# Biases as a feature of layer norm 2, and 64x64 quarters in the slice attention of a fused graph attention and slice attention kernel

## The chip, the cores and the metric

The kernel runs on one core of a Trainium2 chip. A core has four engines that compute, each with its own queue of instructions: TensorE (PE in the profile, with its weight loads as PEld), VectorE (DVE), ScalarE (ACT) and GpSimd (POOL). SyncE (SP) issues DMA transfers. Matmuls write to PSUM, the other tiles lie in SBUF. The metric is the device time of one execution in microseconds, and the median of several executions is given.

## The reference

The input `x` has 32 items of 512 nodes with 256 features, all float32. One layer is two blocks with a residual each. The first is a graph attention network on a layer norm of `x`. The second, which the change touches, is slice attention on a second layer norm:

```python
x = x + gnn(layernorm(x), adj, ...)        # MLP, attention without mask, MLP, attention with mask
x = x + ffn(layernorm(x), ...)

def layernorm(x):                          # over the 256 features
    return (x - mean(x)) / sqrt(var(x) + 1e-5)

def ffn(x, ...):                           # H = 8 heads, D = 64, G = 64 slices
    fx_mid = (x @ W_fx + b_fx)             # per head: [N, 64]
    x_mid  = (x @ W_x + b_x)
    slice_weights = softmax((x_mid @ W_slice + b_slice) / clip(temperature, 0.1, 5.0))
    slice_norm  = slice_weights.sum(over nodes)
    slice_token = einsum('bhnc,bhng->bhgc', fx_mid, slice_weights) / (slice_norm + 1e-5)
    q, k, v = slice_token @ W_q, slice_token @ W_k, slice_token @ W_v
    attn = softmax(q @ k.T / 8)
    out_x = einsum('bhgc,bhng->bhnc', attn @ v, slice_weights)
    return out_x @ W_out + b_out
```

A layer-normed row sums to zero. So its last feature is minus the sum of the 255 others, and a product with a weight matrix can do without it if the matrix's last row is subtracted from all rows.

## The kernel before

Every operation is recorded under a step name (`norm2`, `w`, `sums`, `tokens`, `att`, `vo`, `gg`, `out` for the second block), and a list scheduler in the kernel then orders the operations of all 32 items on each engine. `TURNS`, `PERIOD`, `HEAD` and `TAIL` are the numbers that rank the steps: the higher the turn, the later. Items overlap, so that one item's small steps stand between large matmuls of the others. `HEAD` and `TAIL` shift the first and the last three items. All operations come from one helper, so one source line stands for them all in the profile, and groups are told apart by their tiles.

W_slice and the temperature are folded into W_x (`weff`, with the bias `beff`), W_q and W_k into `wqk`, W_v and W_out into `wvo`. Heads are handled in pairs: 8 heads make 4 pairs of 2 x 64.

```python
# norm2
xn = new("xn2", [P, NT, D + 1])
nc.gpsimd.memset(xn[:, :, D : D + 1], 1.0)        # a column of ones behind the features
layernorm(x1, xn, "ln2")
# ... transposed to xnT ...

# w: for each of four tiles of 128 nodes
nc.tensor.matmul(pm, xnT[:, k, ts(t)], weff[:, k, :], ...)          # k = 0, 1
nc.vector.tensor_tensor(wt, pm, beff, op=OP.add)
nc.vector.tensor_reduce(mx, w3, axis=AX.X, op=OP.max)
nc.vector.tensor_tensor(w3, w3, mx[...].to_broadcast(...), op=OP.subtract)
nc.scalar.activation(wt, wt, AF.Exp)
# ... sum, reciprocal, product ...

# sums: for each pair of heads
nc.tensor.matmul(pm, w[:, t, ts(p)], xn[:, t, :], ...)              # 257 columns, t = 0..3
nc.vector.tensor_scalar(rn, pm[:, D : D + 1], 1e-5, None, op0=OP.add)
# ... s1 = pm / rn; then
pn = sm_tile([NP, P])
nc.tensor.transpose(pn, s1[:, :, D], ident)
for s in range(2):
    nc.vector.tensor_tensor(nrow[:NP, s], ident[...], pn[...], op=OP.mult)

# tokens: wfx times s1T, 16 matmuls of 128 rows x 64 columns; then b_fx
for a in range(2):
    for s in range(2):
        nc.tensor.matmul(pm[ts(s, C), a::2], bfx[:, ts(a, C)], nrow[:, s, a], ...)

def halves(dst, blocks, src):
    for p in range(NP):
        for s in range(2):
            nc.tensor.matmul(dst[ts(s, G), p, :], blocks[:, p, ts(s, G)], src[:, p, :], ...)

def diagonal(dst, src):
    nc.vector.tensor_copy(dst(0), src(0))
    nc.scalar.copy(dst(1), src(1))

nc.tensor.matmul(pq, wqk, tok, start=True, stop=True)
diagonal(... qbd ..., ... pq ...)
halves(psc, qbd, tok)
# att: softmax over psc into sc;  vo: tok and sc transposed
diagonal(... tokbd ..., ... pt ...)
halves(pa, tokbd, attT)
diagonal(... meanbd ..., ... pa ...)
# gg
for p2 in range(NP // 2):
    pg = mm_tile([P, 2, D])
    for s in range(2):
        p = 2 * p2 + s
        nc.tensor.matmul(pg[:, s, :], meanbd[:, p, :], wvo[:, p, :], start=True, stop=True)
    # ... gg = pg + bout
```

`qbd`, `tokbd` and `meanbd` are block-diagonal: zeroed once at the start, and in each item only the two 64x64 blocks of each pair are written. The matmuls contract over all 128 rows, half of which are zero.

Of the kernel before, what the change touches and what calls it, by code (L numbers as in the profile page):

```python
# [10 lines left out]
OP = mybir.AluOpType  # L11
# [5 lines left out]
    "load": -122.2, "norm1": 78.3, "mlp1": 267.5, "h": 296.1, "factors": 313.0, "p": 323.7,  # L17
    "pv": 324.8, "o1": 324.8, "mlp2": 340.5, "h2": 360.8, "e": 385.5, "p2": 385.7,
    "pv2": 430.7, "norm2": 437.4, "w": 494.8, "sums": 496.8, "s1T": 507.4, "tokens": 549.1,
    "att": 558.0, "vo": 558.2, "gg": 560.3, "out": 593.0,  # L20
}
PERIOD, SPARE = 91.1, 0.01

HEAD = (
    (6, -4, -3, 60, -53, 4, -23, -45, -472, 2, -221, -20, 5, -305, -38, -19, -41, -1, 1, -8, -195,
     -10),
    (30, 8, 50, 2, 2, -82, 15, -145, -199, -303, -27, 8, -12, -2, -60, -10, 0, 0, 67, 37, -53,
     -43),
    (0, 0, 24, -14, -200, -9, -14, 38, -69, -68, -93, -18, 33, 0, -64, 3, -16, -34, -14, 0, -61,
     0),  # L30
)
TAIL = (
    (-3, 1, 8, 12, -103, 59, 0, -11, -97, 0, 0, 24, -57, 61, 1, -29, -30, 0, 24, -32, -1, 2),
    (8, -26, 13, 11, -14, 15, 0, 7, -21, -8, -28, 44, -103, 6, -322, 16, 99, 21, 47, 130, 189,
     192),
    (3, 35, 0, 3, 5, 53, -42, 26, -5, 1, 12, -62, 128, 43, 54, -6, -1, -52, -9, -21, -32, -10),
# [7 lines left out]
P = 128  # L44
# [4 lines left out]
class Recorder:  # L49
# [39 lines left out]
    def take(self, engine, method, args, kwargs):  # L89
# [6 lines left out]
        op.half = engine == "tensor" and outs[0].ap[0][1] == P // 2  # L96
# [26 lines left out]
    def _cost(self, op, out, ins):  # L123
# [10 lines left out]
        if op.engine == "tensor":  # L134
            one = max(n / 1200 + 0.002, 0.109)
            if op.half:
                one = max(n / 2400, 0.038)
            return (one if op.method == "transpose" else 2 * one), self.DRAIN
# [13 lines left out]
    def _schedule(self, ops, key, spare):  # L152
# [34 lines left out]
        done, moved, half = [], 0.0, False  # L187
        while len(done) < len(ops):
# [21 lines left out]
            if op.engine == "tensor" and op.half != half:  # L210
                t, half = t + self.SWITCH, op.half
# [102 lines left out]
def adj_ffn_kernel(  # L314
# [61 lines left out]
    Q = 32  # L376
# [106 lines left out]
    bfx = new("bfx", [P, P])  # L483
    nc.gpsimd.memset(bfx, 0.0)
    nc.sync.dma_start(bfx[:NP], b_fx.rearrange("(p f) -> p f", p=NP))
    nrow = new("nrow", [P, 2, 2, NP // 2, G])
    nc.gpsimd.memset(nrow, 0.0)
# [10 lines left out]
    tokbd = new("tokbd", [P, NP, P])  # L498
    nc.gpsimd.memset(tokbd, 0.0)
    qbd = new("qbd", [P, NP, P])  # L500
    nc.gpsimd.memset(qbd, 0.0)
    meanbd = new("meanbd", [P, NP, P])
    nc.gpsimd.memset(meanbd, 0.0)

# [3 lines left out]
    beff = new("beff", [P, INNER])  # L508
# [47 lines left out]
    bxc = new("bxc", [P, NP])  # L556
    nc.sync.dma_start(bxc, b_x.rearrange("(m p) -> p m", p=P))
    bsl = new("bsl", [P, G])
    nc.sync.dma_start(bsl, bcast_dram(b_slice, G))
    for k in range(KD):  # L560
        pt = tr_tile([P, INNER])
        for p in range(NP):
            nc.tensor.transpose(pt[:, ts(p)], wx[:, k, ts(p)], ident)
        wxT = row("u")
        nc.scalar.copy(wxT, pt)
        pw = mm_tile([P, INNER])
        for p in range(NP):
            nc.tensor.matmul(pw[:, ts(p)], wxT[:, ts(p)], ws2, start=True, stop=True)
        nc.vector.tensor_tensor(
            weff[:, k, :].rearrange("p (h g) -> p h g", g=G),  # L570
            pw.rearrange("p (h g) -> p h g", g=G), rtemp_b, op=OP.mult,
        )
    pb = mm_tile([P, INNER])
    for p in range(NP):
        bxb = row("m", (P, P))
        nc.vector.tensor_copy(bxb, bxc[:, p : p + 1].to_broadcast([P, P]))
        nc.tensor.matmul(pb[:, ts(p)], bxb, ws2, start=True, stop=True)
    beff3 = beff.rearrange("p (h g) -> p h g", g=G)
    nc.vector.tensor_tensor(
        beff3, pb.rearrange("p (h g) -> p h g", g=G),  # L580
        bsl[:, None, :].to_broadcast([P, HEADS, G]), op=OP.add,
    )
    nc.vector.tensor_tensor(beff3, beff3, rtemp_b, op=OP.mult)
# [10 lines left out]
    nc.sync.dma_start(wo, W_out.rearrange("(k p) f -> p k f", p=P))  # L594
# [7 lines left out]
    def layernorm(src, dst, name):  # L602
# [9 lines left out]
        for t in range(NT):  # L612
            nc.vector.tensor_scalar(
                dst[:, t, :D], src[:, t, :], mv[:, t, 0:1], rstd[:, t : t + 1],
                op0=OP.subtract, op1=OP.mult,
            )
# [230 lines left out]
    def back(b, x1):  # L847

        nc.step = "norm2"
        xn = new("xn2", [P, NT, D + 1])  # L850
        nc.gpsimd.memset(xn[:, :, D : D + 1], 1.0)
        layernorm(x1, xn, "ln2")
# [16 lines left out]
        for t in range(NT):  # L869
            pm = mm_tile([P, INNER])  # L870
            for k in range(KD):
# [5 lines left out]
            nc.vector.tensor_tensor(wt, pm, beff, op=OP.add)  # L877
            mx = small("mx", [P, HEADS])
            nc.vector.tensor_reduce(mx, w3, axis=AX.X, op=OP.max)
            nc.vector.tensor_tensor(  # L880
                w3, w3, mx[:, :, None].to_broadcast([P, HEADS, G]), op=OP.subtract
# [18 lines left out]
        s1 = new("s1", [P, NP, D + 1])  # L900
        if by_dma("s1", b):
            stage = new("s1_stage", [P, D // Q, P], tag="stage4")
        for p in range(NP):
            pm = mm_tile([P, D + 1])
# [5 lines left out]
            nc.vector.tensor_scalar(rn, pm[:, D : D + 1], 1e-5, None, op0=OP.add)  # L910
            nc.vector.reciprocal(rn, rn)
            nc.vector.tensor_scalar(s1[:, p, :], pm, rn, None, op0=OP.mult)
            if by_dma("s1", b):
                flip(s1[:, p, :D], stage[:, :, ts(p, Q)])

        pn = sm_tile([NP, P])
        nc.tensor.transpose(pn, s1[:, :, D], ident)
        for s in range(2):
            nc.vector.tensor_tensor(
                nrow[:NP, s], ident[:NP, None, s:NP:2, None].to_broadcast([NP, 2, 2, G]),  # L920
                pn.rearrange("j (a o g) -> j a o g", a=2, o=1).to_broadcast([NP, 2, 2, G]), op=OP.mult,
            )
# [22 lines left out]
        pm = mm_tile([P, NP, G])  # L945
        for p in range(NP):
            for k in range(KD):
                for s in range(2):
                    pair, a = p // 2 * 2 + s, p % 2
                    nc.tensor.matmul(  # L950
                        pm[ts(s, C), p, :].rearrange("c (a i) -> c a i", i=Q),
                        wfx[:, k, ts(2 * pair + a, C)],
                        s1T[:, k, :].rearrange("p (a n i) -> p n a i", n=NP, i=Q)[:, pair, ts(a, 2)],
                        start=(p == 0 and k == 0), stop=False,
                    )
        for a in range(2):
            for s in range(2):
                nc.tensor.matmul(
                    pm[ts(s, C), a::2], bfx[:, ts(a, C)], nrow[:, s, a], start=False, stop=(a == 1)
                )  # L960
        nc.joint = False

        def halves(dst, blocks, src):

            nc.joint = True
            for p in range(NP):
                for s in range(2):
                    nc.tensor.matmul(
                        dst[ts(s, G), p, :], blocks[:, p, ts(s, G)], src[:, p, :],
                        start=True, stop=True,  # L970
                    )
            nc.joint = False

        def diagonal(dst, src):
            nc.vector.tensor_copy(dst(0), src(0))
            nc.scalar.copy(dst(1), src(1))

        tok = new("tok", [P, NP, G])
        nc.vector.tensor_copy(tok, pm)
        pq = mm_tile([P, NP, G])  # L980
        nc.tensor.matmul(pq, wqk, tok, start=True, stop=True)
        diagonal(lambda s: qbd[ts(s, C), :, ts(s, G)], lambda s: pq[ts(s, C), :, :])
        psc = sm_tile([P, NP, G])
        halves(psc, qbd, tok)
        nc.step = "att"
        amax = small("amax", [P, NP])
        nc.vector.tensor_reduce(amax, psc, axis=AX.X, op=OP.max)
        sc = new("sc2", [P, NP, G])
        nc.vector.tensor_tensor(
            sc, psc, amax[:, :, None].to_broadcast([P, NP, G]), op=OP.subtract  # L990
        )
        nc.scalar.activation(sc, sc, AF.Exp, scale=C ** -0.5)
        ra = small("ra", [P, NP])
# [3 lines left out]
            sc, sc, ra[:, :, None].to_broadcast([P, NP, G]), op=OP.mult  # L997
# [3 lines left out]

        pt = tr_tile([P, NP, C])
        for q in range(NP // 2):
            nc.tensor.transpose(pt[:, ts(q, 2), :], tok[:, ts(q, 2), :], ident)
        diagonal(lambda a: tokbd[ts(a, G), :, ts(a, C)], lambda a: pt[ts(a, G), :, :])
        pt = tr_tile([P, NP, G])
        for q in range(NP // 2):
            nc.tensor.transpose(pt[:, ts(q, 2), :], sc[:, ts(q, 2), :], ident)
        attT = new("attT", [P, NP, G], tag="sc2")
        nc.scalar.copy(attT, pt)  # L1010
        pa = mm_tile([P, NP, G])
        halves(pa, tokbd, attT)
        diagonal(lambda s: meanbd[ts(s, C), :, ts(s, G)], lambda s: pa[ts(s, C), :, :])
        nc.step = "gg"
        gg = med("gg")
        for p2 in range(NP // 2):
            pg = mm_tile([P, 2, D])
            for s in range(2):
                p = 2 * p2 + s
                nc.tensor.matmul(pg[:, s, :], meanbd[:, p, :], wvo[:, p, :], start=True, stop=True)  # L1020
# [86 lines left out]
```

## Time and profile before

| | |
|---|---|
| median of 3 executions | 2642.68 us (2642.13 to 2643.70) |
| granted TensorE clock, mean | 0.996 |
| TensorE idle before its first matmul | 8.65 us |
| DMA, mean rate | 142 GB/s |

In a line of a group stand: source line, engine, operation, tiles (written, then read), shape, count, then the time in which at least one of them ran, the mean duration of one, and the engine's idle time just before them with what ended it. A line of the timeline has the start, the time to the last end, the engine, the operation and its count. The recorded duration of a matmul contains its way through the pipeline, so that successive matmuls overlap.

### The profile page before, as it was taken

How to read it: one execution, taken by the hardware profiler on the slowest of the kernel's cores; microseconds unless marked ns; L12 is line 12 of the kernel's file. 1: busy time of each engine (PE TensorE's matmuls, PEld its weight loads, DVE VectorE, ACT ScalarE, POOL GpSimd, SP SyncE). 2: the span in 40 equal slices, each digit the busy share in tenths (PEclk: the TensorE clock that was granted, in tenths of full speed). 3: DMA queues.
4: the chain of work that ended last, by engine and by line, in shares of the span. 5: the costliest groups of instructions: out<-in, count | busy, mean ns of one | idle time of the engine just before them, and what ended most of it. 6: DMA issues, size and time to landing. Idle time of an engine off the chain costs nothing.

```text
span 2642.6 us, 35411 instructions
## 1 busy us (share of the span) xinstructions
PE 2601.8 (98%) x12477; PEld 1927.5 (73%) x12477; DVE 2093.8 (79%) x5161; ACT 1082.1 (41%) x2009; POOL 91.2 (3%) x171
## 2 busy tenths in 40 slices
PE   7999999999999999999999999999999999999998
PEld 5777777776777777777777777777777777777775
DVE  6578777987778877779877788877798777898785
ACT  3443444433444434444434444344444334443342
POOL 1000000000000000000000000000000000000000
PEclk9999999999999999999999999999999999999998
DMA  5135455544455554555545555545554545654441
GB/s 164 45 89 154 111 161 169 167 145 133 131 166 168 147 153 126 147 170 167 144 140 139 152 168 152 158 127 143 170 161 143 149 130 152 173 155 143 117 118 37
DMA packets 465658, 375.42 MB, mean 142 GB/s; under 512 B 86596, under 2 KB 382664, under 8 KB 465480
## 3 DMA queue, kind: packets, MB, share of 16 engines
q1 hardware_dynamic: 463896, 372.10, 49.4%
q8 instruction: 99, 1.62, 0.2%
q10 hardware_dynamic: 1584, 1.05, 0.1%
q14 instruction: 79, 0.65, 0.1%
HBM read 197.96 MB, written 175.11 MB: 141 GB/s over the span
## 4 chain that ended last, share of the span: by engine, by line
PE 75%; DVE 12%; DMA 8%; ACT 3%; issue 1%; SPq 1%; DVEq 0%; ACTq 0%
PE mm L277 72%; PE tr L277 3%; DMA w_raw<-scr 3%; DVE pT L277 2%; DMA o1T<-scr 2%; DMA scr<-u_stage 2%; ACT m L277 1%; DVE s L277 1%; DVE s_stage L277 1%; DVE w L277 1%; ACT acb L277 1%; SPq L277 1%; DVE u L277 1%; DVE w_stage L277 1%; DVE acb L277 1%
## 5 line engine op out<-in xcount | busy, mean ns | idle before, releaser
L277 PE MATMUL mm<-wfc,o0T 128*128 128x257 f32 x2048 | 495.6, 381 | 0.0
L277 PE MATMUL mm<-h,pT 128*128 128x256 f32 (+1 forms) x2048 | 466.8, 382 | 8.5 <-DVE pT L277 8.4
L277 PEld LDWEIGHTS mm<-h,pT 128*128 128x128 f32 x2048 | 381.5, 190 | 81.0 <-DVE pT L277 20.4
L277 PEld LDWEIGHTS mm<-wfc,o0T 128*128 128x128 f32 x2048 | 377.9, 189 | 83.7 <-issue 36.1
L277 PE MATMUL mm<-xn,w 128*128 128x257 f32 x1024 | 250.2, 380 | 1.5 <-DVE w L277 1.5
L277 ACT COPY h<-mm 128x257 f32<-128x257 f32 (+1 forms) x384 | 143.1, 373 | 257.8 <-PE mm L277 254.5
L277 PE MATMUL mm<-gg,wT 128*128 128x256 f32 x1024 | 248.5, 379 | 0.0
L277 PE MATMUL mm<-h,p2T 128*128 128x257 f32 x1024 | 241.8, 380 | 0.0
L277 PE MATMUL mm<-xnT,w 128*128 128x512 f32 x512 | 240.1, 602 | 1.0 <-ACT xnT L277 1.0
L277 PE MATMUL mm<-weff,xn2T 128*128 128x512 f32 x512 | 232.7, 596 | 0.0
L277 PE MATMUL mm<-o1T,w 128*128 128x512 f32 x512 | 226.8, 595 | 4.8 <-DVE o1T L277 4.6
L277 PEld LDWEIGHTS mm<-gg,wT 128*128 128x128 f32 x1024 | 191.7, 190 | 36.7 <-issue 12.4
L277 PEld LDWEIGHTS mm<-h,p2T 128*128 128x128 f32 x1024 | 193.3, 189 | 29.1 <-issue 0.6
L277 PEld LDWEIGHTS mm<-xn,w 128*128 128x128 f32 x1024 | 189.3, 190 | 30.9 <-ACT wT L277 1.3
L277 ACT ACTIVATE w<-w 128x512 f32<-128x512 f32 x128 | 80.6, 630 | 307.3 <-DVE w L277 307.1
L277 ACT ACTIVATE u<-mm,rd 128x256 f32<-128x256 f32 x192 | 89.6, 467 | 269.5 <-PE mm L277 149.0
L277 PEld LDWEIGHTS mm<-o1T,w 128*128 128x128 f32 x512 | 95.9, 190 | 116.6 <-issue 87.7
L277 DVE STREAM_TRANSPOSE o_stage<-o2T 128x512 f32<-128x512 f32 x64 | 45.2, 709 | 166.8 <-ACT o2T L277 166.8
L277 PEld LDWEIGHTS mm<-weff,xn2T 128*128 128x128 f32 x512 | 95.6, 191 | 98.0 <-issue 87.6
L277 DVE SCALAR_TENSOR_TENSOR e<-tr,h,mbias 128x512 f32<-128x512 f32 x120 | 86.4, 740 | 98.6 <-PE tr L277 98.6
L277 DVE SCALAR_TENSOR_TENSOR u<-m,u 128x512 f32<-128x512 f32 x192 | 129.7, 686 | 35.0 <-ACT m L277 33.5
L277 PEld LDWEIGHTS mm<-xnT,w 128*128 128x128 f32 x512 | 92.7, 191 | 86.5 <-issue 71.1
(151 smaller groups left out, 3769.8 us busy)
## 6 DMA issues: line engine op xcount, KB each, us to landing
scr<-xn_stage SPq DMA_DIRECT2D x240, 128.0 KB, 2.8
scr<-u_stage SPq DMA_DIRECT2D x120, 256.0 KB, 4.1
o1T<-scr SPq DMA_DIRECT2D x30, 1024.0 KB, 5.7
scr<-e_stage SPq DMA_DIRECT2D x120, 256.0 KB, 3.8
p2T<-scr SPq DMA_DIRECT2D x30, 1024.0 KB, 5.7
scr<-w_stage SPq DMA_DIRECT2D x120, 256.0 KB, 4.5
w_raw<-scr SPq DMA_DIRECT2D x30, 1024.0 KB, 6.3
x<-in_x_dram SPq DMA_DIRECT2D x32, 512.0 KB, 5.4
```

Source lines behind the costliest of these rows:

```text
L277: getattr(getattr(self.nc, op.engine), op.method)(*op.args, **op.kwargs)
```

## The change

Three things are done together. First, the normalised rows keep 255 features, and the last of the 256 becomes a one. `W_fx` and `W_x` have their last row subtracted from all rows in the setup, and their last row is then replaced by the bias. So the biases come with the product: `beff`, `bfx`, `nrow`, the transpose of the norms and the 257th column go. Second, the attention among slices and the product with W_v W_out work on 64x64 quarters of TensorE's array, without the block-diagonal tiles and their zeros. Third, the scheduler's numbers are new, and it knows the quarters as a mode of their own.

```diff
 TURNS = {
-    "load": -122.2, "norm1": 78.3, "mlp1": 267.5, "h": 296.1, ...
+    "load": -742.6, "norm1": -217.3, "mlp1": 743.3, "h": 847.3, ...
 }
-PERIOD, SPARE = 91.1, 0.01
+PERIOD, SPARE = 91.72, 0.01
 # ... HEAD and TAIL: all new
+    def less_last(w, source, bias):
+        last = row("m")
+        nc.sync.dma_start(last, bcast_dram(source[D - 1], INNER))
+        for k in range(KD):
+            nc.vector.tensor_tensor(w[:, k, :], w[:, k, :], last, op=OP.subtract)
+        nc.sync.dma_start(w[P - 1 : P, KD - 1, :], bias.rearrange("(p f) -> p f", p=1))
+    less_last(wfx, W_fx, b_fx)
 # ... and less_last(wx, W_x, b_x); setup of bfx, nrow, beff, bxc, the block-diagonal tiles: gone
-        xn = new("xn2", [P, NT, D + 1])
-        nc.gpsimd.memset(xn[:, :, D : D + 1], 1.0)
-        layernorm(x1, xn, "ln2")
+        xn = new("xn2", [P, NT, D])
+        nc.gpsimd.memset(xn[:, :, D - 1 : D], 1.0)
+        layernorm(x1, xn, "ln2", D - 1)
-            nc.vector.tensor_tensor(wt, pm, beff, op=OP.add)
-            nc.vector.tensor_reduce(mx, w3, axis=AX.X, op=OP.max)
+            nc.vector.tensor_reduce(mx, pm3, axis=AX.X, op=OP.max)
             nc.vector.tensor_tensor(
-                w3, w3, mx[:, :, None].to_broadcast([P, HEADS, G]), op=OP.subtract
+                w3, pm3, mx[:, :, None].to_broadcast([P, HEADS, G]), op=OP.subtract
             )
-            pm = mm_tile([P, D + 1])
+            pm = mm_tile([P, D])
-        pn = sm_tile([NP, P])
-        nc.tensor.transpose(pn, s1[:, :, D], ident)
-        for s in range(2):
-            nc.vector.tensor_tensor(nrow[:NP, s], ...)
-        for a in range(2):
-            for s in range(2):
-                nc.tensor.matmul(
-                    pm[ts(s, C), a::2], bfx[:, ts(a, C)], nrow[:, s, a], start=False, stop=(a == 1)
-                )
-        def halves(dst, blocks, src):
-        ...
-        def diagonal(dst, src):
-        ...
+        q = new("q", [P, 2, 2, G])
+        nc.scalar.copy(q, pq)
+        def quarters(dst, left, right):
+            nc.joint = True
+            for j in range(2):
+                for r in range(2):
+                    for c in range(2):
+                        nc.tensor.matmul(
+                            dst(r, c, j), left(r, c, j), right(r, c, j), start=True, stop=True
+                        )
+            nc.joint = False
+        psc = [sm_tile([P, 2, G]) for s in range(2)]
+        quarters(
+            lambda s, a, d: psc[s][ts(a, G), d, :],
+            lambda s, a, d: q[ts(s, C), a, d, :],
+            lambda s, a, d: tok[ts(s, C), a, d, :],
+        )
 # ... the softmax in two halves up to its exponential; tokT and attT transposed whole
+        pa = [mm_tile([P, 2, G]) for d in range(2)]
+        quarters(
+            lambda d, a, s: pa[d][ts(a, C), s, :],
+            lambda d, a, s: tokT[ts(d, G), a, ts(s, C)],
+            lambda d, a, s: attT[ts(d, G), s, ts(a, G)],
+        )
+        mean = new("mean", [P, 2, 2, G])
+        nc.vector.tensor_copy(mean[:, 0], pa[0])
+        nc.scalar.copy(mean[:, 1], pa[1])
-        for p2 in range(NP // 2):
-            pg = mm_tile([P, 2, D])
-            for s in range(2):
-                p = 2 * p2 + s
-                nc.tensor.matmul(pg[:, s, :], meanbd[:, p, :], wvo[:, p, :], start=True, stop=True)
+        pg = [mm_tile([P, 2, D]) for a in range(2)]
+        quarters(
+            lambda a, s, d: pg[a][ts(s, G), d, :],
+            lambda a, s, d: mean[ts(a, C), d, s, :],
+            lambda a, s, d: wvo[ts(a, C), 2 * d + s, :],
+        )
```

In `quarters`, `r` is the half of the array's rows and `c` the half of its columns. Each row half writes a PSUM tile of its own.

## The prediction

> **What bounds the kernel now.** I read the page's busy shares first, then the chain that ended last.
>
> ```profile
> PE 2601.8 (98%) x12477; PEld 1927.5 (73%) x12477; DVE 2093.8 (79%) x5161; ACT 1082.1 (41%) x2009; POOL 91.2 (3%) x171
> ...
> PE 75%; DVE 12%; DMA 8%; ACT 3%; issue 1%; SPq 1%; DVEq 0%; ACTq 0%
> ```
>
> TensorE (PE) is busy 98% of the span and makes up 75% of the chain. A busy PE could still be a slow one, so I looked at when its instructions start. Each fp32 matmul stands in the trace as two passes. Inside a run of equal passes the median distance of two starts is 216 ns at 257 columns, 429 ns at 512 and 109 ns for a 128-column transpose: all are columns / 1.2 GHz plus about 2 ns. In a steady item PE does nothing but stream, and what the change is worth is the PE time it takes out. VectorE (79%) and ScalarE (41%) have room. The same transpose of two successive items starts at 1303.91 and 1384.48 us: 80.6 us an item, 32 items 2578 us, the rest being head and tail.
>
> Next the groups by shape that the change touches (count, then busy us, mean ns):
>
> ```profile
> L277 PE MATMUL mm<-wvo,meanbd 128*128 128x256 f32 x256 | 72.7, 390 | 0.3 <-ACT meanbd L277 0.3
> L277 PE MATMUL mm<-s1T,wfx 128*64 128x64 f32 x1024 | 37.4, 226 | 3.7 <-DMA s1T<-scr 3.7
> L277 PE MATMUL tr<-tok,qbd 128*64 128x64 f32 x512 | 23.3, 231 | 1.6 <-DVE qbd L277 1.4
> L277 PE MATMUL mm<-attT,tokbd 128*64 128x64 f32 x512 | 21.9, 228 | 0.5 <-ACT attT L277 0.5
> L277 PE MATMUL mm<-nrow,bfx 128*64 128x128 f32 x256 | 20.3, 278 | 0.1
> ...
> L277 PE MATMUL tr<-ident,s 128*4 128x128 f32 x32 | 8.7, 271 | 0.0
> ```
>
> The mean of one (222 to 390 ns) contains the pipeline's latency, so the cost is not count times mean. It is the distance from one start to the next, which the timeline of one steady item gives (start us, then us from the first start to the last end):
>
> ```profile
> 1319.28 1.15 PE L277 MATMUL mm<-s1T,wfx 128*64 128x64 f32 x32
> 1320.26 0.61 PE L277 MATMUL mm<-nrow,bfx 128*64 128x128 f32 x8
> 1320.80 2.84 PE L277 MATMUL mm<-xnT,w 128*128 128x512 f32 x6
> ...
> 1325.72 0.69 PE L277 MATMUL tr<-tok,qbd 128*64 128x64 f32 x16
> 1326.33 0.44 PE L277 MATMUL tr<-ident,tok 128*128 128x128 f32 x2
> ...
> 1332.53 0.69 PE L277 MATMUL mm<-attT,tokbd 128*64 128x64 f32 x16
> 1333.15 1.13 PE L277 MATMUL mm<-wfc,o0T 128*128 128x257 f32 x4
> ```
>
> The 16 passes on qbd hold PE from 1325.72 to 1326.33, 0.61 us. Their single starts alternate 7 and 52 ns apart: the left and the right half of the array start 7 ns apart, and the next pair follows when the first has streamed its 64 columns. So 15 distances take 0.46 us, and the last one, on leaving for a 128x128 pass, 0.15. Entering a half-array group costs the pass before it a median 96 ns more than its columns, leaving one 99 ns more: about 0.195 us a visit, 99 visits in the run.
>
> **What the Trainium skill says.** "TensorEngine Tiling (Array Packing)", Key Properties: 64x64 gives four tiles that load weights and multiply independently, and a change of tiling mode drains TensorE. The trace agrees for two tiles (7 ns between the halves' starts) and puts the drain at 0.195 us a visit; no run here shows four tiles yet. "TensorE: Matmul & The Clock Gate", Part 3, has a pack span of one matmul plus about 4 ns per further tile; here it is 7 per tile. "TensorEngine Tiling (Array Packing)", Gotcha 1, says that different row tiles must not access one PSUM bank at the same time. The changed code gives each row half its own PSUM tile (`psc[s]`, `pa[d]`, `pg[a]`), so the four can overlap; before shows no row tiles. "TensorE: Matmul & The Clock Gate", Part 1, says that an idle PE falls to a lower clock; the tail of before shows it (0.72, below).
>
> **The change part by part, per item.**
> 1. Bias matmuls `nrow x bfx`: 8 passes go. Their pairs start 105 ns apart, 4 x 105 = 0.42, and with the step into them 0.44 us. The leaving switch now follows the tokens, so it is not saved.
> 2. The transpose of the norms (`s`, 4 columns of weights): 109 ns, 0.11 us.
> 3. `qbd` halves become `q` quarters: 16 passes remain, but four tiles run. Rounds of four: 4 x 52 ns, plus 3 x 7 ns within the last round, is 0.18 to the last start, plus 0.15 to leave: 0.35 instead of 0.61. Saved 0.26.
> 4. `tokbd` halves become `tokT` quarters: the same, 0.26.
> 5. Gates `meanbd x wvo`: 8 passes on the full array over block-diagonal weights of which half is zero. They start a mean 233 ns apart (216, and 320 where the weights were waited for): 1.87. After: 16 quarter passes of 256 columns in four rounds of 213 ns, 0.85, plus 0.02 of stagger, plus a new visit, 0.195: 1.07. Saved 0.80. This is the largest term and the least tested one.
> 6. Sums with 256 instead of 257 columns: 32 passes x 0.8 ns, 0.03.
>
> Sum 1.90 us an item, 61 us for 32 items. All of it lies on PE, which has no slack, so all of it should count.
>
> Off the path: VectorE loses the 128 additions of `beff` (84.8 us), 64 `nrow` products (24.3), and `qbd` and `tokbd` copies (13.2 + 13.0) in the whole run, while the subtraction and the maximum now read PSUM. In the profile reductions and additions of the same 512 columns take 663 to 683 ns whether from PSUM or SBUF, so this is free. VectorE comes to about 1970 us, even further from being the bound; the 0.33 us for pT that 25 items wait for it may shrink.
>
> **The new turns.** The order of instructions in the changed program shows the steady item much as before, with tighter fits behind the small groups: one 512-column matmul (0.86 us) between the q product and the quarters that need it (0.43 us for the product's own two passes, and a copy of 0.37 us plus latencies must fit in 1.29 us), and one `wfc` matmul (0.43) instead of two between `pa` and the gates, where two copies of 0.28 us run side by side. I allow 0.1 us of new waiting an item, 3 us.
>
> In the head, item 0's whole `h` now comes before its maximum, and W_v W_out after it. Before:
>
> ```profile
> PE mm L277 <- DVE pT L277: 8.4, 25, 4.0
> ```
>
> The longest pT wait, 4.0 us, is in the head, 5.7 us after the `fm` transpose at 40.88 us. The wo matmuls (8 x 0.216 = 1.73, with a wait of 0.5) and the bias setup (8 x 0.11) no longer stand ahead of `fm`: about 3 us earlier. The subtraction of W_x's last column and its bias row are on the way to `weff`; W_x's transposes stand behind 12 and 21 more matmuls and should not wait.
>
> In the tail:
>
> ```profile
> 2575.12 4.94 PE L277 MATMUL mm<-h,p2T 128*128 128x257 f32 x22
> 2583.76 1.45 PE L277 MATMUL mm<-s1T,wfx 128*64 128x64 f32 x32 [3.69 <-DMA s1T<-scr]
> ...
> 2591.54 2.43 PE L277 MATMUL tr<-ident,xn 128*128 128x128 f32 x8 [0.32 <-DVE xn L277]
> ...
> 2580.00:2604.00 24.00, 17.14 (x92) 9.11 (x92) 16.18 (x41) 6.44 (x14) 1.26 (x2) 0.72 0.07 23
> ```
>
> Between the last item's p2 product and its second norm PE has only small things to do; the clock falls to 0.72 (the last line is a window's busy times, then the clock). The new order puts two `weff` matmuls (1.7 us) and 16 of the sums (6.9) of the item before into this 11.5 us hole and takes the tokens' small work (about 3 us) out of it: about 5 us gained, clock included.
>
> Together: 2642.7 - 61 - 3 - 5 + 3 = 2577 us.
>
> **Rivals.** *Row tiles don't overlap in fp32.* Then quarters run as pairs, like the halves: terms 3 to 5 vanish, and a visit of 0.195 is added. Left are 0.44 + 0.11 + 0.03 - 0.2 = 0.4 us an item, 12 us, and the 5 us of the turns: about 2625. For it: no row tile is in the profile of before. Against: column halves overlap exactly as described, and the banks are separate. I give it one in eight. *A new wait takes the place of the work removed.* The chain tokens, q, softmax, attention, means, gates is serial, and there is less work to hide it behind. For it: the fits above. If each of its five steps waited 0.2 us, 32 us return: about 2606. Against: in the steady items of before PE hardly waits inside this chain (1.4 us in three waits for qbd, 0.5 in one for attT), and the chain gets shorter by the serial copies of `qbd`, `tokbd` and `meanbd` on two engines. *VectorE or DMA becomes the bound.* It would stop the gain at their busy time, about 1970 us or half the DMA share, far from it.
>
> **Range and chances.** The steady sum is good to some 8 us if quarters overlap; turns, head and tail add some 8 either way; the rivals lengthen the upper side. 2556 to 2604. The 2% line is at 2590, 13 us above the middle: faster 0.80, same 0.17, slower 0.03.
>
> **What would show it.** Right: quarter groups whose four starts lie some 7 ns apart; the q and pa groups hold PE about 0.35 us and the gates about 1.07; the period is near 78.7 us; 128 visits to tiled modes; no nrow or beff rows; the first p product some 3 us earlier. Wrong: quarter starts 7 and 52 apart, or 107 ns a pass in the gates; steady waits of PE for q, mean or sc; idle time in the tail as before.

## The result, and the profile after

The changed kernel takes 2585.89 us (median of four executions, 2581.80 to 2586.01) against 2642.65: a ratio of 0.978, 95% interval 0.9765 to 0.9793. It is faster by 57 us where the prediction had 66, and lies inside the predicted range.

The page of the changed kernel: busy shares, and shares of the chain.

```profile
PE 2543.5 (98%) x12437; PEld 1863.3 (72%) x12437; DVE 1992.3 (77%) x4968; ACT 1075.3 (42%) x2009; POOL 90.5 (4%) x167
...
PE 84%; DVE 7%; DMA 6%; ACT 1%; SPq 1%; issue 1%; POOL 0%; DVEq 0%; ACTq 0%
```

TensorE is as full as before, 98%, and its part of the chain has grown. VectorE has 101.5 us less to do. The groups that answer to those of before:

```profile
L283 PE MATMUL mm<-s1T,wfx 128*64 128x64 f32 x1024 | 37.1, 225 | 0.0
L283 PE MATMUL mm<-wvo,mean 64*64 64x256 f32 x512 | 35.0, 389 | 0.0
...
L283 PE MATMUL tr<-tok,q 64*64 64x64 f32 x512 | 14.8, 230 | 0.0
L283 PE MATMUL mm<-attT,tokT 64*64 64x64 f32 x512 | 14.8, 230 | 0.0
```

The gates now have 512 passes and are busy 35.0 us; they had 256 and 72.7. The two quarter groups went from 23.3 and 21.9 to 14.8 each. The groups of `nrow` and of the 4-column transposes are gone. One steady item on the timeline:

```profile
1304.34 1.02 PE L283 MATMUL mm<-xnT,w 128*128 128x512 f32 x2
1305.30 0.46 PE L283 MATMUL tr<-tok,q 64*64 64x64 f32 x16
1305.69 0.44 PE L283 MATMUL tr<-ident,tok 128*128 128x128 f32 x2
...
1310.60 0.46 PE L283 MATMUL mm<-attT,tokT 64*64 64x64 f32 x16
1310.99 0.70 PE L283 MATMUL mm<-wfc,o0T 128*128 128x257 f32 x2
1311.62 1.09 PE L283 MATMUL mm<-wvo,mean 64*64 64x256 f32 x16
1312.64 2.87 PE L283 MATMUL mm<-wfc,o0T 128*128 128x257 f32 x12
```

From the start of a q group to the next full-array pass is 0.39 us (it was 0.61), from the start of the gates 1.02. The trace's single starts show the four tiles. Counted from the first start of a group, the median q passes start at 0, 7, 13, 20 ns, then at 107, 113, 120, 127, and two more rounds begin at 165 and 223; the rounds of the gates begin at 0, 267, 482 and 698, again with four starts within 20 ns. So, after a longer first round, four passes run per round of 58 ns at 64 columns and of 216 ns at 256.

To see where all of the time went I divided the span of each profile by the starts of TensorE's passes. *Stream*: each pass on the full array counts as its columns / 1.2 GHz plus 2.5 ns. *Tiled*: the distance from a pass on a part of the array to the next start, so that leaving the mode is in it. *Over*: what the distances after full-array passes have beyond their stream, that is waits, entering a mode, weights not yet loaded, a low clock. What is left is before the first pass and after the last start.

| profile | span | lead | stream | tiled | over | tail |
|---|---|---|---|---|---|---|
| before | 2642.6 | 8.7 | 2461.2 | 93.2 | 75.5 | 4.2 |
| after | 2584.1 | 8.3 | 2400.7 | 95.1 | 75.8 | 4.2 |

The gain is stream: the gates left the full array, and the tiled groups, which took them in, did not grow, because the bias passes left and the others became quarters. "Over" is the same in sum, but not in place: in the first 52 us it went from 12.6 to 9.9, in the last 105 us from 14.4 to 7.5, and in between from 48.5 to 58.3. Of these 9.8 us more in between, 8.1 stand ahead of the products on o1T (below), some 5 are what the additional visits to a tiled mode cost outside "tiled", and other waits lost about 4. The tail's hole is filled as foreseen. In the last items of the changed kernel:

```profile
2519.57 7.11 PE L283 MATMUL mm<-h,p2T 128*128 128x257 f32 x32
2526.52 1.88 PE L283 MATMUL mm<-weff,xn2T 128*128 128x512 f32 x4
2528.24 5.34 PE L283 MATMUL mm<-xn,w 128*128 128x256 f32 x24
2534.35 1.97 PE L283 MATMUL mm<-xn,w 128*128 128x256 f32 x8 [0.77 <-DVE ln_mv L283]
2537.80 1.40 PE L283 MATMUL tr<-ident,xn 128*128 128x128 f32 x8 [1.49 <-DVE xn L283]
```

TensorE streams for most of the way from the last p2 product to the last norm's transposes. A window's clock there (2526.5 to 2540) is 1.00 where before had 0.72. What TensorE waits for, in the middle of the kernel, is o1T:

```profile
PE mm L283 <- DVE o1T L283: 10.5, 10, 1.9
...
PE mm L283 <- DVE pT L283: 4.7, 4, 4.0
```

In before the same row read:

```profile
PE mm L277 <- DVE o1T L277: 4.6, 6, 2.2
```

By the starts (a distance beyond the stream of its first pass), some 20 items lose 14.5 us ahead of the o1T products; before, some 10 items lost 6.4 us. For pT the two readings differ: the row went from 25 times to 4, but by the starts 25 items lose 7.6 us ahead of the pT products, and 24 lost 8.2 before. Losses of 0.3 us leave idle times that are mostly too short to be listed, so this wait has not shrunk.

### The profile page after: what moved, and what is told of

Same layout as the page of the kernel before. It is cut to its first block, busy times and chain, and to the rows that moved or that the text cites. A ratio compares the mean times of both kernels' runs of the same rounds, so it can differ in the third digit from the quotient of the medians.

```text
span 2584.1 us, 35267 instructions
## 1 busy us (share of the span) xinstructions
PE 2543.5 (98%) x12437; PEld 1863.3 (72%) x12437; DVE 1992.3 (77%) x4968; ACT 1075.3 (42%) x2009; POOL 90.5 (4%) x167
## 3 DMA queue, kind: packets, MB, share of 16 engines
q8 instruction: 99, 1.62, 0.3%
## 4 chain that ended last, share of the span: by engine, by line
PE 84%; DVE 7%; DMA 6%; ACT 1%; SPq 1%; issue 1%; POOL 0%; DVEq 0%; ACTq 0%
PE mm L283 81%; PE tr L283 3%; DMA o1T<-scr 2%; DMA scr<-u_stage 2%; SPq L283 1%; DVE s L283 1%; DVE s_stage L283 1%; DVE acb L283 1%; ACT acb L283 1%; DVE pT L283 1%; DVE u L283 1%; DMA w_raw<-scr 1%; DVE w L283 0%; DVE u_stage L283 0%; DMA p2T<-scr 0%
## 5 line engine op out<-in xcount | busy, mean ns | idle before, releaser
L283 PE MATMUL mm<-wfc,o0T 128*128 128x257 f32 x2048 | 509.8, 382 | 0.0
L283 PE MATMUL mm<-h,pT 128*128 128x257 f32 (+1 forms) x2048 | 462.1, 382 | 8.2 <-DVE pT L283 4.7
L283 PE MATMUL mm<-weff,xn2T 128*128 128x512 f32 x512 | 248.7, 592 | 0.6 <-ACT xn2T L283 0.6
L283 PE MATMUL mm<-xn,w 128*128 128x256 f32 x1024 | 247.5, 380 | 0.9 <-DVE ln_mv L283 0.8
L283 PE MATMUL mm<-gg,wT 128*128 128x256 f32 x1024 | 237.5, 380 | 0.1
L283 PEld LDWEIGHTS mm<-xnT,w 128*128 128x128 f32 x512 | 93.2, 191 | 83.4 <-issue 77.0
L283 ACT ACTIVATE m<-m 128x512 f32<-128x512 f32 x192 | 120.0, 625 | 66.9 <-DVE m L283 66.7
```

Of the source, the lines that this page charges most:

```text
L283: getattr(getattr(self.nc, op.engine), op.method)(*op.args, **op.kwargs)
```

## The experiments

Four questions: whether the turns or the operations carry the gain, whether VectorE's relief counts, whether the four tiles depend on how the products are queued, and what the o1T wait is worth.

**Operations and turns, crossed.** The scheduler's numbers (TURNS, PERIOD, HEAD, TAIL) are exchanged as one block. "Bias only" takes the bias feature and leaves halves and block-diagonal tiles.

```diff
 # before with new turns
-TURNS = {"load": -122.2, ...}; PERIOD, SPARE = 91.1, 0.01; HEAD, TAIL = ...
+TURNS = {"load": -742.6, ...}; PERIOD, SPARE = 91.72, 0.01; HEAD, TAIL = ...
 # after with old turns: the reverse, in the changed kernel
```

> The kernel before with the scheduler's numbers of after, nothing else. Theory A (the gain is TensorE work taken out; the turns are worth a few us in head and tail): 2630 to 2660 us, for the turns were fitted to other operations, so the steady items may even wait more. Rival B (the new turns carry much of the gain): under 2620 us.

> The operations of after with the scheduler's numbers of before. Theory A: the small groups' saving of about 53 us stays (measured 1.65 us an item), head and tail are not improved: 2585 to 2602 us. Rival B (turns): over 2615 us.

```diff
 # bias only, on the kernel before, with either set of turns
+    less_last(wfx, W_fx, b_fx)            # and wx
-            nc.vector.tensor_tensor(wt, pm, beff, op=OP.add)
-        nc.tensor.transpose(pn, s1[:, :, D], ident)      # and the nrow products
-                nc.tensor.matmul(pm[ts(s, C), a::2], bfx[:, ts(a, C)], nrow[:, s, a], ...)
```

> Before with the biases in layer norm 2's last feature alone; block-diagonal halves and turns as before. Theory A: 0.44 + 0.11 + 0.03 us an item less on TensorE, 19 us: 2620 to 2627 us. Rival C (VectorE's relief by 109 us shortens TensorE's waits): under 2612 us, with the waits for pT and o1T gone.

> Bias feature, halves, and the turns of after. Theory A: 2615 to 2640 us; the distance to after (2586) is the quarters' share, 0.22 + 0.22 + 0.64 us an item, about 35 us. Rival B: within 15 us of after.

| operations | turns | us | ratio to before (95%) | stream | tiled | over |
|---|---|---|---|---|---|---|
| before | new | 2929.92 | 1.108 (1.106 to 1.111) | 2461.2 | 120.0 | 334.2 |
| after | old | 2645.52 | 1.000 (0.999 to 1.001) | 2400.7 | 105.5 | 125.0 |
| bias only | old | 2751.71 | 1.041 (1.039 to 1.042) | 2455.9 | 102.8 | 177.4 |
| bias only | new | 2952.48 | 1.117 (1.116 to 1.119) | 2455.9 | 106.7 | 380.9 |

Only one expectation was met: rival B's for after with old turns. The run beside it contradicts B too, for there the new turns cost 287 us instead of helping, and the other three runs missed every number given. The stream is what the operations say, whatever the turns: 2461.2, 2455.9 or 2400.7. But a set of turns that was not made for the operations adds 50 to 305 us of "over". New turns on the operations before, for instance, stall the sums behind the softmax:

```profile
PE mm L279 <- DVE w L279: 116.8, 62, 2.4
PE mm L279 <- DMA p2T<-scr: 35.2, 27, 3.0
```

and old turns on the operations after spread small waits over many items:

```profile
PE mm L281 <- DVE tok L281: 10.6, 19, 1.6
...
PE mm L281 <- DVE ex L281: 5.2, 24, 0.3
PE mm L281 <- ACT o0T L281: 3.6, 23, 0.2
```

So the new turns carry no gain of their own, and the new operations lose theirs under the old turns. These runs can't say what one part of the change is worth, since each has a new order. That called for runs in which the order is held.

**One part at the order of before.** The scheduler still sees the operations left out and ranks them, but they are not issued; TensorE's order is that of before without them.

```diff
+            if op.ghost:
+                continue
 # no bias matmuls: ghosts are the norms' transpose, the nrow products, the bfx matmuls
 # no beff: the ghost is the addition; mx and the subtraction read pm in place of wt
```

> The kernel before at its own order of instructions, with the bias matmuls (8 passes), the transpose of the norms and the nrow products left out: b_fx is not added. Theory A (at a fixed order TensorE's time counts one to one): 0.44 + 0.11 us an item, 18 us less: 2621 to 2630 us. Rival C (what counts is VectorE): no gain beyond 6 us. Rival D (with the turns no longer fitted, waits eat the gain, as in the two bias-only runs): over 2640 us.

> The kernel before at its own order, with the addition of beff left out and maximum and subtraction reading PSUM: VectorE has 85 us less. Theory A: VectorE is not the bound, 2638 to 2645 us. Rival C: under 2632 us.

Without the bias matmuls: 2632.35 us against 2642.64, ratio 0.9966 (0.9953 to 0.9978). That is 10 us less and in none of the ranges given: 2 us above theory A's, too much for C and too little for D's. In its profile stream and tiled fall by 3.5 + 12.7 = 16.2 us, close to the 18 expected, but "over" rises by 6.4, and 9.5 us of the span remain as gain. Three rows of its waits (total us, times, longest):

```profile
PE mm L281 <- DVE pT L281: 8.5, 25, 4.0
PE mm L281 <- DVE tok L281: 5.6, 10, 1.6
PE mm L281 <- DVE o1T L281: 4.7, 9, 1.1
```

The waits for pT and o1T are those of before (8.4 and 4.6). The one for tok has doubled; it was, before:

```profile
PE mm L277 <- DVE tok L277: 2.9, 5, 1.3
```

By the starts, the distance from the 512-column products on xnT to the q product (wqk, on tok) after them grew by 3.7 of the 6.4 us, the largest part; the rest is spread. This fits work that had hidden part of the way from the tokens to q. Theory A holds for the work and not for the end, where waits eat a part, as D says.

Without the addition of beff: 2647.82 us, ratio 1.0021 (1.0011 to 1.0031), stream and tiled as before, "over" 76.3. VectorE's busy time:

```profile
PE 2601.1 (98%) x12477; PEld 1926.8 (73%) x12477; DVE 2029.4 (77%) x5033; ACT 1081.5 (41%) x2009; POOL 91.2 (3%) x171
```

It falls by 64 us, not by the 85 of the group, since the recorded times of successive instructions overlap. The kernel is 5 us slower, 3 us above theory A's range, so this relief of VectorE is worth nothing: rival C falls. No run takes the quarters alone at a held order. Their share of the gain, the larger one, is read from the starts and not isolated by an experiment.

**How the quarters are queued.** The loops of `quarters` in another order.

```diff
 # row halves in turn            # tile by tile
-for j in range(2):             -for j in range(2):
-    for r in range(2):         -    for r in range(2):
-        for c in range(2):     -        for c in range(2):
+for r in range(2):             +for r in range(2):
+    for j in range(2):         +    for c in range(2):
+        for c in range(2):     +        for j in range(2):
```

> After, with the eight matmuls of each quarter group ordered by row half first: only the two column tiles alternate. Theory A (four tiles overlap because neighbours in the queue are on different tiles): pairs as in the halves, 0.2 + 0.2 + 0.75 us an item more, 37 us: 2615 to 2632 us. Rival E (the engine picks from its queue, the order does not matter): within 4 us of 2586.

> After, with both matmuls of one tile behind each other, then the next tile. Theory A: passes of one tile follow at its streaming time, only at the border of two tiles do two overlap: gates 2.8 to 3.5 us instead of 1.03, q and pa 0.85 to 0.95 instead of 0.39, together 86 to 115 us: 2668 to 2704 us. Rival E: within 4 us of 2586.

They take 2612.90 us (ratio 0.9896, 0.9881 to 0.9911) and 2611.64 (0.9891, 0.9876 to 0.9905). Rival E's time, within 4 us of 2586, is missed by both. The first lies just below theory A's 2615, the second far below its 2668: the cause is another. Groups of the second run:

```profile
L283 PE MATMUL mm<-wvo,mean 64*64 64x256 f32 x512 | 35.7, 389 | 0.5 <-DVE mean L283 0.5
L283 PE MATMUL tr<-tok,q 64*64 64x64 f32 x512 | 15.6, 233 | 0.5 <-ACT q L283 0.5
```

The quarters cost little more than in after (35.0 and 14.8): from first start to leaving a q group takes 392 ns in after, 406 with row halves in turn and 413 tile by tile. All of "tiled" is 98.7 and 99.4 against 95.1 us. Still four passes run per round, and only the steps inside a round differ: 7, 7, 7 ns in after, 7, 20, 7 with row halves in turn, 13, 13, 13 tile by tile. That fits about 6.6 ns for each place in the queue from one tile's product to the next tile's. A product whose tile is busy costs its place, but does not hold up one on a free tile. Rival E is right on the quarters, apart from these 14 to 21 ns a group. The lost time is "over" (100.7 and 97.7 instead of 75.8), and most of it is one wait, early in the kernel. The first run's timeline:

```profile
271.01 0.59 PE L283 MATMUL mm<-xn,w 128*128 128x256 f32 x2
286.06 1.98 PE L283 MATMUL mm<-s1T,wfx 128*64 128x64 f32 x32 [14.45 <-DMA s1T<-scr]
```

In the second run the same wait is 14.43 us. Both runs have one order outside the quarters, in which, by their tiles, 423 of TensorE's 12437 passes stand at another place than in after. There the tokens came before their s1T had gone through DRAM.

**The o1T wait.** First comes the changed kernel again, on the chip of the runs that follow. Then two local moves in the finished order, and then a change of the ranking.

```diff
 # h pulled: PULL = (("mlp2", "h"),); h and p2 pulled: also ("pv", "pv2")
+        # before the first product of step `first`, the rest of the open PSUM group of step `other`
+        ops = ops[:i] + rest + [op for op in ops[i:] if op not in rest]
 # mlp2 later
+                    if step == "mlp2":
+                        keys[op] += 1.8
```

> The changed kernel once more, on the chip of the next three: 2582 to 2587 us.

> After, with one local move in the finished order: the rest of an open group of h products (three matmuls as a rule, 1.3 us) goes ahead of the o1T products of mlp2. Theory F (what the changed kernel gave up is a fit: its small groups hide 1.6 us less of the path of o1T through DRAM, so PE waits for it): the 14.5 us that are lost ahead of o1T go down by 8 to 12 us, 2573 to 2579 us. Rival G (the chain behind o1T is as tight: what is hidden ahead is waited for after): within 3 us of after.

> As the run before, and the one outstanding product of an open p2T group goes ahead of the first pT product (0.43 us against a wait of 0.3 us in 25 items, 7.6 us in all). Theory F: another 3 to 7 us less, 2568 to 2576 us. Rival G: no more than 2 us less.

> After, with mlp2's turn 1.8 us later in the ranking that the list scheduler works from, so that the whole order is made anew. Theory F: as good as the local move, 2573 to 2582 us, if the scheduler changes nothing else. Rival H (any change of the ranking disturbs places that were fitted): 2588 us or more.

| run | us (range) | ratio to before (95%) | over |
|---|---|---|---|
| after again | 2583.33 (2582.96 to 2584.72) | 0.9782 (0.9768 to 0.9795) | 73.1 |
| h pulled | 2583.56 (2582.03 to 2585.25) | 0.9782 (0.9768 to 0.9795) | 72.7 |
| h and p2 pulled | 2580.16 (2578.72 to 2581.57) | 0.9769 (0.9756 to 0.9783) | 69.1 |
| mlp2 later | 2606.08 (2603.74 to 2608.41) | 0.9867 (0.9853 to 0.9880) | 92.3 |

The repeat lies where it was expected. With h pulled the o1T wait is all but gone from the waits:

```profile
PE mm L301 <- DVE o1T L301: 0.4, 1, 0.4
```

and the time is the same. By the starts, the 10.9 us ahead of o1T (after again) have become 0.9, and instead 7.6 us stand between the transposes of h2 (none in after again) and 4.7 inside the h2 products (0.7), a few steps further on. The path from o1T through mlp2 and h2 to the mask is as tight behind as ahead: rival G. With both moves the time is 3.2 us below after again and 3.4 below h pulled. That is in theory F's 3 to 7 us for the second move, though its range of times is missed: the 7.5 us that 25 items lost ahead of pT go, and some 3 us more are lost inside the pT products. This is the fastest version here; its range does not touch that of after on the same chip, though the two ratios to before overlap. The re-ranked order lost 23 us, of which one wait for s1T early in the kernel (at 270 us) is 13.0: rival H. Why just that place gives way in two different orders, this one and that of the loop runs, stays open.

## Why the prediction was right, by its own steps

*What bounds.* Right. TensorE stays at 98%; the relief of VectorE alone gave nothing. VectorE's busy time came to 1992.3 us where some 1970 was expected.

*Steps 1 and 2, biases and norms.* Predicted 0.55 us an item; left out at a fixed order, stream and tiled fell by 16.2 us, 0.51 an item.

*Steps 3 and 4, q and attention quarters.* Four tiles did run. Predicted 0.35 us a group, measured 0.39. The terms given make 0.33: up to the last start there are three distances between rounds, not four. Each is 58 ns, not 52, as the pairs of before are too (7 + 52), and the second round starts 107 ns after the first. In the group shown above, the first round's weight loads start together with its passes (1305.294 and 1305.295 us), which then last 267 ns instead of 218; the later rounds' weights are loaded ahead. The halves of before have the same first step, 100 ns from the second start to the third; with it their 15 distances make 0.46 us, without it only 0.42. Saved 0.22 each, not 0.26.

*Step 5, gates.* The largest term. Predicted 1.07 us with the visit, measured 1.02 from start to leaving, plus 0.096 for entering, plus a cost that the visit of 0.195 us left out: after leaving, the second full-array pass starts about 0.105 us late (321 ns after the first instead of 216). The first one's weights are not loaded ahead either: after the gates shown above their load starts 2 ns before it, and it lasts 484 ns instead of 380. A visit is rather 0.3 us. So 1.23 us, and 0.64 saved instead of 0.80.

Corrected, the sum is 0.40 + 0.11 + 0.22 + 0.22 + 0.64 + 0.03 = 1.62 us an item or 52 us, where the prediction had 61. The account of the two profiles agrees: stream and tiled fall by 58.6, and 29 more visits (128, as predicted, after 99), at 0.2 us each outside "tiled", give back 6.

*The period.* Predicted near 78.7 us. From the fifth item to the 27th the wqk products start a mean 79.29 us apart, before 80.51. That is 1.22 us an item, not 1.90. In the least disturbed items the period was 80.2 us and is 78.6 to 78.7, which is close to the corrected sum. What the mean saves less than that is waiting, most of it ahead of o1T.

*The new turns.* The head's first p product starts at 43.45 us instead of 46.54, the 3 us predicted, but not just along with `fm`: that transpose came 4.9 us earlier (36.01 us instead of 40.88), and the way from it to p grew from 5.7 to 7.4 us. The wait before p is still 4.04 us. The tail gained 6.9 us, 5 predicted. New steady waits were allowed 3 us, at q and at the gates. Those fits held: no wait for q, sc or mean to speak of. The wait came at o1T, 8.1 us more than before in the profiled run, 4.5 in the repeat. The prediction looked for it in the chain whose work was cut, and it stood in another, from o1T to the mask. Why that chain now waits longer is argued, from the order and from the run without the bias matmuls, and not shown by itself.

*The sum.* Steps 52, head 3, tail 7 and o1T -8 make 54 of the 58.5 us between the two profiles; the other 4 or so are spread over small terms. The prediction's 66 had the steps 9 us too high, the new waits 5 us too low and the tail 2 us too low. That the total came so close is thus in part luck; the mechanism, passes taken off a full TensorE, is not.

*What it weighed wrongly.* It took the turns for a few microseconds: 3 and 5 gained at the ends, 3 lost in between, and some 8 either way. With the turns of before, the same operations gain nothing. It read from the order that the new turns suited, but gave no weight to how much they must.

*Tiles and their order.* In the Trainium skill, what "TensorEngine Tiling (Array Packing)", Key Properties, says of independent tiles is borne out: four of them start 7 ns apart. "TensorE: Matmul & The Clock Gate", Part 3, says that matmuls keep strict program order; the steps of 13 and 20 ns with unchanged rounds speak against it between the tiles of these fp32 products, though the trace does not name the tile of a start.

## What to carry to other kernels

When one engine streams without a break, count what a change takes out of it by the distance from start to start, not by durations, and count entering and leaving a tiling mode with what follows it. What an operation hides for others is lost with it: taking 16 us of small matmuls out at a fixed order gave 10. A wait that is removed at one place can come back a few steps on, as behind o1T. And with a list scheduler whose ranks were fitted, a part of a change can't be judged by a rebuild alone; hold the order, and read stream and waits separately.

## What the runs showed that was not expected

Both products of a 64x64 tile can stand behind each other in the queue, and still four tiles run: the second delays the next tile's by about 6.6 ns and does not stop it. Entering, leaving and the first weights after a tiled group cost about 0.3 us a visit. One transfer's place in the order cost 13 to 14.5 us once, after changes that touch none of it.
